# Reordering the start of a fused gated cross-attention and feed-forward kernel: first scores behind half of the projections, weight sums behind the scores, all of w_o held back

## The chip, the cores and the metric

The kernel runs on one core of a Trainium2 chip. The metric is device time in microseconds, as the median of several executions. One more execution was profiled by the hardware; its own time and its span (first to last instruction) are given beside each other below. The matrix engine is called PE, the vector engine DVE, the scalar engine ACT, GpSimd POOL, and the queue that issues most DMAs SP.

## What is computed

There are 16 batches of 224 tokens with 512 channels. Each batch has 750 context rows of 384 channels, of which a mask drops some. Cut to what matters:

```python
x = x + tanh(g0) * xattn(layernorm(x), ctx, mask)   # 8 heads of 64
x = x + tanh(g1) * ffn(layernorm(x))

def xattn(x, ctx, mask):
    q = x @ W_q;  k = ctx @ W_k;  v = ctx @ W_v      # split into heads
    p = softmax(where(mask, q k^T / 8, -max))
    return (p v) @ W_o + b_o

def ffn(x):                                          # 512 -> 2048 -> 512
    h = gelu(bitlinear(x, w1, b1))
    return bitlinear(h, w2, b2)

def bitlinear(x, w, b):
    s = 1 / mean(|w|)                                # one number for a whole matrix
    wq = clip(round(w * s), -1, 1) / s               # ternary weights
    return act_quant(rmsnorm(x)) @ wq.T + b
```

The ternary weights can only be formed when a whole matrix has been read, since their scale is the mean of its absolute values.

## The kernel before

The kernel ranks the batches by how many context rows the mask keeps, and gathers only those rows (at most 192 for a batch of the first half, 128 for the second). A batch in this order has a number `s` from 0 to 15. The path that runs is `compact_path`; its pieces, with their lines:

- `fetch` and `gather` (L936, L848) are indirect DMAs, issued by POOL, for token rows and context rows. `select(s)` (L807) makes the row numbers of batch `s`: six comparisons on DVE (`ind`, L814), twelve small matmuls (`pi`, L820), two conversions on DVE (`keys`, L831).
- `norm(i)` (L942) normalises two tiles of 128 tokens: statistics on DVE (`bs_x`, `mv_x`, L950 and L951), the rest on POOL (L954 to L959). The first two tiles have their own form, `norm_first` (L963).
- `query_pieces(s)` (L997) holds the transposes `turn` (`xnp`, L985) and two halves of the query projection (`qp_0`, `qp_2`, L1006). `context_pieces(s)` (L865) holds two transposes (`ctxp`, L879), two halves of the key projection (`kp_0`, `kp_2`, L890), the values (`vp`, L905) and the values of the rows past 128 (`vr`, L916). A result in PSUM is copied out by `evict` (L755), on DVE (L761) or ACT (L764), whichever has less planned work by a running estimate, `load`.
- `scores(s, n)` (L1035) is a quarter of a batch's scores: four matmuls `sim` (L1045), a masked maximum for each head on DVE (L1059), an exponential on ACT (L1069), a reciprocal on DVE (`rec`, L1078), a product on POOL (L1079). Quarters 0 and 1 need only the first half of the queries and of the keys. `turn_probs` (L1089) transposes the result (`ptp`, `ptr`), and `weighted` (L1113) applies it to the values.
- The weights: `load_weights` (L1338) brings w1 in eight pieces of 512 KB; w2 follows piece by piece into the same buffers as these come free. `sum_weights` (L1352) sums the absolute values of a piece, even ones on DVE (`wsums`, L1359), odd ones on ACT (`junk`, L1363). `scale_weights` (L1367) adds the eight sums (`wtot`, L1369), spreads the total by a matmul (`wtotp`, L1371) and makes the scale `sw`. `round_weights` (L1388) makes a ternary piece in three passes of DVE (L1392, L1393, L1394), and `turn_weights` (L1397) transposes it (`wp`, L1405 for w1, L1409 for w2).
- `late_loads` (L229) loads b_o, b2, W_o and b1 by SP. A copy of one element into a destination, made by ACT after the last weight sum (L1482 and L1483), holds such a load back until w1 has been summed. Of W_o, only the piece in slots 0 and 1 (L236) is held so; slots 2 and 3 (L237 and L238, 256 KB each) are not.

Every engine runs its instructions in the order of its own queue. That order is made when the program is built: a scheduler takes instructions in the order in which the Python code names them, and lets one pass another where it believes it to be ready sooner. `tc.issue_after(ins)` puts what is named inside the block behind `ins` on the queue of `ins`'s engine. It adds no wait on another engine.

The start of the work is written out by hand; from then on `merge` (L1430) interleaves three streams by estimated cost: the attention of batch `s`, the preparation of batch `s + 1`, and either the weights (s = 0 for w1, s = 1 for w2) or the feed-forward of finished token tiles.

Of the kernel before, what the change touches and what calls it, by code (L numbers as in the profile page):

```python
# [725 lines left out]
def compact_path(ctx, tc, sh, x, context, out, late_loads):  # L726

    nc = tc.nc
    P = 128
    B, S, D = x.shape  # L730
    _, J, C = context.shape
# [20 lines left out]

    load = {"v": 0.0, "s": 0.0}

    def evict(dst, src, cols):  # L755

        kind = {"saturate": False} if dst.dtype == F8 else {}
        v, s = 80 + 1.2 * cols, 90 + 1.0 * cols
        if load["v"] + v <= load["s"] + s:
            load["v"] += v  # L760
            nc.vector.tensor_copy(dst, src, **kind)  # L761
        else:
            load["s"] += s
            nc.scalar.copy(dst, src, **kind)  # L764

    def gen(shape, dtype, name):
        return ps_gen.tile(shape, dtype, tag="gen", name=name)
# [36 lines left out]
    def rows_of(s, t):  # L804
        return min(CAPS[s] - t * P, P)

    def select(s):  # L807

        st = live[s]
        cap = CAPS[s]  # L810
        nt = 2 if cap > P else 1
        ind = pa.tile([TJ, NJ, 192], BF16, tag="ind", name=f"ind_{s}", bufs=1)
        for n in range(NJ):
            nc.vector.tensor_scalar(ind[:, n, :cap], sh.place[:TJ, :cap], sh.upto[:, n, s : s + 1], None, ALU.is_ge)  # L814
        load["v"] += 6 * 170
        pi = gen([P, 2], F32, f"pi_{s}")
        for t in range(nt):
            rows = rows_of(s, t)
            for n in range(NJ):
                nc.tensor.matmul(  # L820
                    pi[:rows, t : t + 1],
                    lhsT=ind[:, n, t * P : t * P + rows],
                    rhs=sh.one[:, 0:1],
                    start=(n == 0),
                    stop=(n == NJ - 1),
                )

        keys = pa.tile([P, 2], I32, tag="keys", name=f"keys_{s}", bufs=3)
        for t in range(nt):
            rows = rows_of(s, t)  # L830
            nc.vector.tensor_scalar(  # L831
                keys[:rows, t : t + 1],
                pi[:rows, t : t + 1],
                float(J - 1),
                sh.first[:rows, s : s + 1],
                ALU.min,
                ALU.add,
            )
        st["keys"] = keys

        mb = pa.tile([TQ, 320], F32, tag="mask", name=f"mask_{s}", bufs=1)
        nm = 320 if nt > 1 else P
        nc.vector.tensor_scalar(
            mb[:, :nm], sh.place_f[:TQ, :nm], sh.slots[:TQ, 0, s : s + 1], -FMAX, ALU.is_ge, ALU.mult
        )
        st["mask"] = mb
# [18 lines left out]
    def context_pieces(s):  # L865
        st = live[s]
        cap = CAPS[s]
        nt = 2 if cap > P else 1

        def trans(c0, c1):  # L870
            if c0 == 0:
                st["ctxT"] = pa.tile([P, NC, 192], F32, tag="ctxT", name=f"ctxT_{s}", bufs=1)
                st["kT"] = pa.tile([P, NP, 320], F32, tag="kT", name=f"kT_{s}", bufs=2)
                st["v"] = pa.tile([P, D], F32, tag="v", name=f"v_{s}", bufs=2)
            pt = gen([P, c1 - c0, cap], F32, f"ctxp_{s}_{c0}")
            for c in range(c0, c1):
                for t in range(nt):
                    rows = rows_of(s, t)
                    nc.tensor.transpose(  # L879
                        pt[:, c - c0, t * P : t * P + rows],  # L880
                        st["ctx"][:rows, t, c * P : (c + 1) * P],
                        ident[:rows, :rows],
                    )
            evict(st["ctxT"][:, c0:c1, :cap], pt, (c1 - c0) * cap)

        def keys(p0):
            pk = gen([P, 2, cap], F32, f"kp_{s}_{p0}")
            for p in (p0, p0 + 1):
                for c in range(NC):
                    nc.tensor.matmul(  # L890
                        pk[:, p - p0, :],
                        lhsT=sh.wk[:, c, p * P : (p + 1) * P],
                        rhs=st["ctxT"][:, c, :cap],
                        start=(c == 0),
                        stop=(c == NC - 1),
                    )
            evict(st["kT"][:, p0 : p0 + 2, :cap], pk, 2 * cap)
            if cap > P:

                evict(st["kT"][DH:, p0 : p0 + 2, 192:], pk[DH:, :, :P], 2 * P)  # L900

        def values():
            pv = gen([P, D], F32, f"vp_{s}")
            for c in range(NC):
                nc.tensor.matmul(  # L905
                    pv, lhsT=st["ctxT"][:, c, :P], rhs=sh.wv[:, c, :], start=(c == 0), stop=(c == NC - 1)
                )
            evict(st["v"], pv, D)

        def values_rest():  # L910

            pv = gen([P, NP, DH], F32, f"vr_{s}")
            for c in range(NC):
                by = sh.wv[:, c, :].rearrange("p (i j d) -> p i j d", j=2, d=DH)
                for j in range(2):
                    nc.tensor.matmul(  # L916
                        pv[j * DH : (j + 1) * DH],
                        lhsT=st["ctxT"][:, c, P:],
                        rhs=by[:, :, j, :],
                        start=(c == 0),  # L920
                        stop=(c == NC - 1),
                    )
            st["v_rest"] = pa.tile([P, NP, DH], F32, tag="v_rest", name=f"v_rest_{s}", bufs=2)
            evict(st["v_rest"], pv, D // 2)

        pieces = [(0.5 * nt, lambda: trans(0, 2)), (0.3 * nt, lambda: trans(2, 3))]
        pieces += [(0.01 * cap, lambda p=p: keys(p)) for p in (0, 2)]
        pieces.append((1.5, values))
        if nt > 1:
            pieces.append((0.8, values_rest))  # L930
        return pieces
# [65 lines left out]
    def query_pieces(s):  # L997
        st = live[s]

        def query(p):  # L1000
            if p == 0:
                st["qT"] = pa.tile([P, NP, S], F32, tag="qT", name=f"qT_{s}", bufs=2)
            pq = gen([P, 2, S], F32, f"qp_{s}_{p}")
            for i in range(2):
                for d in range(ND):
                    nc.tensor.matmul(  # L1006
                        pq[:, i, :],
                        lhsT=sh.wq[:, d, (p + i) * P : (p + i + 1) * P],
                        rhs=st["xnT"][:, d, :],
                        start=(d == 0),  # L1010
                        stop=(d == ND - 1),
                    )
            evict(st["qT"][:, p : p + 2, :], pq, 2 * S)

        pieces = [(0.4, lambda t=t: turn(t)) for t in tiles_of(s)]
        pieces += [(3.0, lambda p=p: query(p)) for p in (0, 2)]
        return pieces
# [5 lines left out]
    def norm_pieces(s):  # L1023
        pieces = []
        for t in tiles_of(s):
            if t % 2 == 0:
                pieces.append((0.0, lambda t=t: norm(t // 2)))
                if t // 2 + 2 < NTOK // 2:
                    pieces.append((0.0, lambda t=t: fetch(t // 2 + 2)))
        return pieces  # L1030
# [302 lines left out]
    NPC = FF * D // P // W  # L1333
    sh.isw = [None, None]
    raws = {}
    weight_sums = []
# [15 lines left out]
    def sum_weights(wi, c):  # L1352
        if c == 0:
            weight_sums.append(pa.tile([P, NPC], F32, name=f"wsums_{wi}"))
        if c == 1:
            late["junk"] = pa.tile([P, FF], F32, tag="h", name=f"junk_{wi}", bufs=2)
        raw = raws[wi, c]
        if c % 2 == 0:
            nc.vector.tensor_reduce(  # L1359
                weight_sums[wi][:, c : c + 1], raw, AX.X, ALU.add, apply_absolute_value=True  # L1360
            )
        else:
            nc.scalar.activation(late["junk"][:, :W], raw, AF.Abs, accum_out=weight_sums[wi][:, c : c + 1])  # L1363
# [106 lines left out]
    with tc.issue_after(load_weights(0, 0)):  # L1470
        for c in range(1, NPC):
            load_weights(0, c)
    for piece in query_pieces(0) + context_pieces(0):
        piece[1]()
    for _, piece in norm_pieces(1):
        piece()
    select(2)
    for c in range(NPC):
        sum_weights(0, c)
    scale_weights(0)  # L1480

    for dst in (sh.wo[0:1, 0, 0:1], sh.bo[0:1, 0:1], sh.b1[0:1, 0:1], sh.b2[0:1, 0:1]):  # L1482
        nc.scalar.copy(dst, weight_sums[0][0:1, NPC - 1 : NPC])  # L1483
    late_loads(True)
    scores(0, 0)
    scores(0, 1)

    begun = 0
    for s in range(B):
# [30 lines left out]
    while begun < NPAIR + 2:  # L1520
# [7 lines left out]
        c = up_pieces(i - 1) if i - 1 < NPAIR else []  # L1528
# [34 lines left out]
```

## Time and profile before

| What | Value |
|---|---|
| median of 3 runs | 779.38 us (778.71 to 779.67) |
| the profiled execution: its own time, its span | 781.03 us, 779.2 us |
| mean granted PE clock in it | 0.947 |
| PE busy | 698.1 us, 90% of the span |
| DVE busy | 514.6 us, 66% |
| ACT, POOL busy | 387.4 us (50%), 370.9 us (48%) |
| DMA moved | 58.76 MB, 75 GB/s over the span |

The profile is a page with six parts: busy times; the span in 40 slices of 19.5 us, with a digit for the busy tenths of each engine and for the granted PE clock; DMA queues; the chain of work that ended last; the costliest groups of instructions; DMA issues. From the same trace come lists: the timeline of an engine (start, duration, engine, line, operation, result, operands, count, and in brackets the idle time before it and what ended it; several instructions in a row are merged, with the count as x8), the chain in order of time (start, length, what), the waits of a window, and tables of busy time by window. An fp32 matmul of the program appears as two records. Times are from the start of the span.

### The profile page before, as it was taken

Reading aid. Unit: us, or ns where it says so; the run is one execution under the profiler, and the core shown is the slowest. Engines: PE = TensorE matmul, PEld = TensorE weight load, DVE = VectorE, ACT = ScalarE, POOL = GpSimd, SP = SyncE. Lnnn points to the kernel's source line nnn. Section 1 sums busy time; section 2 is a strip of 40 time slices with the busy share of each in tenths; the row PEclk is TensorE's granted clock in tenths of the full one; section 3 lists DMA queues with packets and bytes.
Section 4 is the critical chain, followed back from the end, with each engine's and each line's share of the span. In section 5 each row is a group of like instructions: output and inputs, shape, how many; then the busy total and the mean of one; then the engine's idle time right before and its main releaser. Section 6 shows DMA issues by size and latency. Waiting matters only on the chain.

```text
span 779.2 us, 11250 instructions
## 1 busy us (share of the span) xinstructions
PE 698.1 (90%) x3902; PEld 446.6 (57%) x3902; DVE 514.6 (66%) x1293; ACT 387.4 (50%) x947; POOL 370.9 (48%) x468
## 2 busy tenths in 40 slices
PE   3698799999998998998999889999998999989762
PEld 2566587666564664664756476666564756443321
DVE  5479774758657539536687825695858576688960
ACT  1248664354826527346374654382728364554330
POOL 6446358453563453535537433555362425254331
PEclk9889989999999798998999979999999999999886
DMA  6855122111311223024133310242312222223331
GB/s 218 299 178 173 33 67 58 30 43 29 82 44 44 73 68 77 16 69 91 41 70 84 90 36 11 69 92 68 66 54 58 53 55 55 68 55 90 83 85 45
DMA packets 87185, 58.76 MB, mean 75 GB/s; under 512 B 75456, under 2 KB 75600, under 8 KB 86992
## 3 DMA queue, kind: packets, MB, share of 16 engines
q1 hardware_dynamic: 78992, 32.00, 18.2%
q0 software_dynamic: 8128, 25.96, 10.6%
q8 instruction: 33, 0.54, 0.3%
q14 instruction: 32, 0.26, 0.1%
HBM read 32.26 MB, written 7.34 MB: 51 GB/s over the span
## 4 chain that ended last, share of the span: by engine, by line
PE 67%; DVE 16%; ACT 5%; issue 4%; DMA 3%; POOL 2%; DVEq 0%; POOLq 0%; ACTq 0%; SPq 0%
PE qp L1006 12%; PE hp L1257 10%; PE fp L1303 10%; PE kp L890 8%; PE op L1187 7%; DVE a L1280 4%; PE vp L905 4%; PE av L1124 4%; PE sim L1045 3%; DVE hq L1283 3%; DVE h L1265 3%; PE ptp L1099 3%; DMA raw<-in_L_ffn_w_dram 2%; ACT h L1277 1%; ACT p L1069 1%
## 5 line engine op out<-in xcount | busy, mean ns | idle before, releaser
L1079 POOL TENSOR_TENSOR p<-p,rec 112x768 f32<-112x768 f32 (+1 forms) x64 | 81.3, 1273 | 151.9 <-DVE rec L1078 99.3
L1265 DVE SCALAR_TENSOR_TENSOR h<-hp,c,b_bc 128x1024 f32<-128x1024 f32 x56 | 71.6, 1281 | 95.2 <-PE hp L1257 95.2
L1257 PE MATMUL hp<-w1T,xqT 128*128 128x512 fp8e4 x448 | 108.7, 389 | 8.0 <-DMA xqT<-xq 5.1
L1069 ACT ACTIVATE p<-p,nm 112x192 f32<-112x192 f32 (+1 forms) x256 | 106.5, 421 | 17.2 <-DVE nm L1059 17.1
L1187 PE MATMUL op<-wo_sb,xoT 128*128 128x512 f32 x224 | 107.4, 618 | 3.3 <-DVE y L1190 3.2
L1303 PE MATMUL fp<-w2T,hqT 128*128 128x512 fp8e4 x448 | 103.0, 386 | 7.5 <-DMA hqT<-hq 7.5
L1006 PE MATMUL qp<-xnT,wq_sb 128*128 128x224 f32 x512 | 106.7, 364 | 2.4 <-ACT xnT L764 2.4
L1006 PEld LDWEIGHTS qp<-xnT,wq_sb 128*128 128x128 f32 x512 | 98.4, 197 | 5.6 <-ACT xnT L764 3.1
L1059 DVE CUSTOM_DVE_ANT_0 p<-sim,mask 112x192 f32<-112x192 f32 (+1 forms) x256 | 69.1, 316 | 24.1 <-PE sim L1045 22.0
L1257 PEld LDWEIGHTS <-xqT 128*128 128x128 bf16 x448 | 43.2, 99 | 64.8 <-issue 18.5
L1303 PEld LDWEIGHTS <-hqT 128*128 128x128 bf16 x448 | 43.9, 99 | 60.5 <-DMA hqT<-hq 9.0
L890 PE MATMUL kp<-ctxT,wk_sb 128*128 128x192 f32 (+1 forms) x384 | 68.3, 330 | 7.9 <-issue 6.0
L1277 ACT ACTIVATE h<-h 128x2048 f32<-128x2048 f32 x28 | 53.5, 1911 | 42.7 <-DVE h L1265 27.6
L890 PEld LDWEIGHTS kp<-ctxT,wk_sb 128*128 128x128 f32 x384 | 62.5, 211 | 15.5 <-issue 8.9
L1045 PE MATMUL sim<-kT,qT 64*112 64x192 f32 (+1 forms) x512 | 56.8, 327 | 12.7 <-DVE nm L1059 12.6
L1187 PEld LDWEIGHTS op<-wo_sb,xoT 128*128 128x128 f32 x224 | 41.9, 197 | 44.9 <-issue 39.1
L1280 DVE TENSOR_REDUCE a<-h 128x1 f32<-128x2048 f32 x28 | 63.6, 2280 | 5.0 <-ACT h L1277 4.9
L791 POOL DMA_INDIRECT x<-in_x_dram,token x28 | 33.8, 1206 | 59.6 <-PE xnp L985 42.0
L1045 PEld LDWEIGHTS sim<-kT,qT 64*112 64x112 f32 x512 | 39.0, 178 | 32.1 <-DVE nm L1059 15.2
L1289 ACT ACTIVATE sq<-h 128x2048 bf16<-128x2048 f32 x28 | 53.1, 1899 | 7.6 <-DMA hqT<-hq 7.6
L764 ACT COPY kT<-kp 128x256 f32<-128x256 f32 (+2 forms) x43 | 17.4, 405 | 79.3 <-PE kp L890 71.3
L764 ACT COPY qT<-qp 128x448 f32<-128x448 f32 x31 | 16.5, 533 | 72.7 <-PE qp L1006 72.7
(167 smaller groups left out, 1161.0 us busy)
## 6 DMA issues: line engine op xcount, KB each, us to landing
raw<-in_L_ffn_w_dram SPq DMA_DIRECT2D x16, 512.0 KB, 4.9
wq_sb<-in_L_xattn_W_q_dram SPq DMA_DIRECT2D x1, 1024.0 KB, 5.7
b_bc<-in_L_ffn_b_dram SPq DMA_DIRECT2D x1, 1024.0 KB, 8.6
wk_sb<-in_L_xattn_W_k_dram SPq DMA_DIRECT2D x1, 768.0 KB, 7.3
wv_sb<-in_L_xattn_W_v_dram SPq DMA_DIRECT2D x1, 768.0 KB, 8.7
wo_sb<-in_L_xattn_W_o_dram SPq DMA_DIRECT2D x2, 256.0 KB, 4.0
wo_sb<-in_L_xattn_W_o_dram SPq DMA_DIRECT2D x1, 512.0 KB, 3.8
x<-in_x_dram,token POOLq DMA_INDIRECT x28, 4.8
```

The lines of the kernel that those rows point to most:

```text
L890: nc.tensor.matmul(pk[:, p - p0, :], lhsT=sh.wk[:, c, p * P : (p + 1) * P], rhs=st["ctxT"][:, c, :cap], start=(c == 0), stop=(c == NC - 1),)
L1006: nc.tensor.matmul(pq[:, i, :], lhsT=sh.wq[:, d, (p + i) * P : (p + i + 1) * P], rhs=st["xnT"][:, d, :], start=(d == 0), stop=(d == ND - 1),)
L1045: nc.tensor.matmul(sim[:, j, i, :cap], lhsT=st["qT"][j * DH : (j + 1) * DH, p, q * TQ : (q + 1) * TQ], rhs=st["kT"][j * DH : (j + 1) * DH, ...
L1059: nc.vector.tensor_tensor_reduce(out=probs[:, h, :cap], in0=sim[:, j, i, :cap], in1=st["mask"][:, j * begin : j * begin + cap], scale=-(DH ...
L1069: nc.scalar.activation(probs[:, h, :cap], probs[:, h, :cap], AF.Exp, bias=nmax, scale=-1.0, accum_out=total[:TQ, h : h + 1],)
L1079: nc.gpsimd.tensor_tensor(probs[:, :, :cap], probs[:, :, :cap], rec[:TQ].unsqueeze(2).to_broadcast([TQ, 4, cap]), ALU.mult,)
L1187: nc.tensor.matmul(po, lhsT=xoT[:, d, at : at + P], rhs=sh.wo[:, d, :], start=(d == 0), stop=(d == ND - 1))
L1257: nc.tensor.matmul(ph[:, n, :], lhsT=f["xqT"][:, k * ND + d, :], rhs=w1T[:, d, at : at + NB], start=(d == 0), stop=(d == ND - 1),)
L1265: nc.vector.scalar_tensor_tensor(h[:, cols], ph.rearrange("t i n -> t (i n)"), f["c1", k], sh.b1[:, cols], ALU.mult, ALU.add)
L1277: nc.scalar.activation(f["h", k], f["h", k], AF.Gelu)
L1280: nc.vector.tensor_reduce(amax[:, k : k + 1], h, AX.X, ALU.max, apply_absolute_value=True)
L1303: nc.tensor.matmul(po, lhsT=f["hqT", k][:, n, :], rhs=w2T[:, n, :], start=(n == 0), stop=(n == NF - 1))
```

## The change

It touches the hand-written start of `compact_path`. `evict` notes the latest eviction on DVE and on ACT. The context transposes of batch 0 come ahead of the token transposes. Then come the first half of the queries and the first half of the keys. All else of the start is queued, on DVE and ACT, behind the latest eviction of each: the two quarters of scores, then the second halves, the values, the sums of w1 and its scale, the normalisation of the next two tiles, the selection for batch 2. Two more one-element copies hold back the other two loads of W_o.

```diff
+    latest = {}
+
     def evict(dst, src, cols):
...
-            nc.vector.tensor_copy(dst, src, **kind)
+            latest["v"] = nc.vector.tensor_copy(dst, src, **kind).ins
...
-            nc.scalar.copy(dst, src, **kind)
+            latest["s"] = nc.scalar.copy(dst, src, **kind).ins
...
-    for piece in query_pieces(0) + context_pieces(0):
-        piece[1]()
-    for _, piece in norm_pieces(1):
+    queries, keys_values = query_pieces(0), context_pieces(0)
+    for _, piece in keys_values[:2] + queries[:2]:
         piece()
-    select(2)
-    for c in range(NPC):
-        sum_weights(0, c)
-    scale_weights(0)
-
-    for dst in (sh.wo[0:1, 0, 0:1], sh.bo[0:1, 0:1], sh.b1[0:1, 0:1], sh.b2[0:1, 0:1]):
-        nc.scalar.copy(dst, weight_sums[0][0:1, NPC - 1 : NPC])
+    for _, piece in queries[2:3] + keys_values[2:3]:
+        piece()
+
+    with ExitStack() as behind:
+        for instruction in latest.values():
+            behind.enter_context(tc.issue_after(instruction))
+        scores(0, 0)
+        scores(0, 1)
+        for _, piece in queries[3:] + keys_values[3:]:
+            piece()
+        for c in range(NPC):
+            sum_weights(0, c)
+        scale_weights(0)
+        for _, piece in norm_pieces(1):
+            piece()
+        select(2)
+
+        held = [sh.wo[0:1, 0, 0:1], sh.wo[0:1, 2, 0:1], sh.wo[P // 2 : P // 2 + 1, 2, 0:1]]
+        for dst in held + [sh.bo[0:1, 0:1], sh.b1[0:1, 0:1], sh.b2[0:1, 0:1]]:
+            nc.scalar.copy(dst, weight_sums[0][0:1, NPC - 1 : NPC])
     late_loads(True)
-    scores(0, 0)
-    scores(0, 1)
```

The queues of the two built programs, compared, differ in these places (before, then after):

- DVE, from the normalisation of tile 1 on. Before: six `ind` of batch 2, `bs_x` of tiles 2 to 5 mixed with `wsums`, the eviction of `ctxp_0` behind five of these six `bs_x` and two `wsums`, the evictions of the keys, `wtot`, the rest of `select(2)`, `sw`, the eight maxima of the scores, the six `ind` of batch 3, the first rounding. After: the eviction of `kp_0`, two `wsums`, the eight maxima, `rec`, a `wsums`, the eviction of `qp_2`, a `wsums`, `rec`, two evictions of `kp_2`, `wtot`, two `bs_x`, six `ind`, the eviction of `vr`, `sw` mixed with two `bs_x`, `keys` and six `ind`, the first rounding.
- PE. Before: `xnp`, `qp_0`, `qp_2`, `ctxp`, `kp_0`, `kp_2`, `vp`, `vr`, `pi`, `wtotp`, `sim` of quarters 0 and 1. After: `ctxp`, `xnp`, `qp_0`, `kp_0`, two matmuls of `qp_2`, `sim` of quarters 0 and 1, the rest of `qp_2`, `kp_2`, `vp`, `vr`, `wtotp`, `pi`.
- ACT. Both evictions of `ctxp` come first; the exponentials of quarter 0 stand ahead of `junk` of piece 5, those of quarter 1 ahead of `junk` of piece 7 and of the one-element copies.
- POOL. The products of quarters 0 and 1 come ahead of the normalisation of tiles 2 and 3, the gather of batch 2 and the two products of biases and gates (L1502, L1503), rather than behind them.
- SP. The loads L237 and L238 move from ahead of w1 to behind b_o and b2, still ahead of b1.
- Later, up to the fourth batch, some ten evictions change between DVE and ACT or change places by a few; after that the queues are the same.

## Prediction, made before the changed kernel ran

> **What bounds the kernel now.** I read first the slices of the page, then the chain in order of time, then the timelines of DVE and PE, then windows.
>
> ```profile
> PE   3698799999998998998999889999998999989762
> PEclk9889989999999798998999979999999999999886
> ```
>
> A digit is a slice of 19.5 us. PE is the bound from the sixth slice to the last three. Below nine it is in the first, second, fourth and fifth: 0 to 97 us. Time saved there stays saved if what follows is bound by PE.
>
> In the chain (start, length, what) the worst place is this:
>
> ```profile
> 32.77 2.89 issue
> 35.66 6.60 PE kp L890 x24
> 42.26 2.58 PE vp L905 x6
> 44.84 1.45 PE vr L916 x12
> ```
>
> PE idles 5.98 us before the keys. Its operand `ctxT` comes from DVE, whose timeline says why it is late:
>
> ```profile
> 30.93 0.69 DVE L950 BATCH_NORM_STATS2 bs_x<-x 128x6 f32<-128x512 f32 x1 [2.42 <-DMA x<-in_x_dram,token]
> 32.69 0.69 DVE L950 BATCH_NORM_STATS2 bs_x<-x 128x6 f32<-128x512 f32 x1 [1.06 <-DMA x<-in_x_dram,token]
> 33.30 1.20 DVE L1359 TENSOR_REDUCE wsums<-raw 128x1 f32<-128x1024 f32 x1
> 34.42 0.68 DVE L950 BATCH_NORM_STATS2 bs_x<-x 128x6 f32<-128x512 f32 x1
> 35.02 0.54 DVE L761 COPY ctxT<-ctxp 128x384 f32<-128x384 f32 x1
> ```
>
> PE made `ctxp` by 29.7. The copy stands behind statistics of later tiles, and these wait for their rows. Then the clock (columns: window, length, busy PE, PEld, DVE, ACT, POOL, granted clock, DMA share, GB/s):
>
> ```profile
> 30.00:35.60 5.60, 0.00 (x0) 0.00 (x0) 3.60 (x6) 1.42 (x4) 1.52 (x2) 0.84 0.85 330
> 35.60:37.60 2.00, 1.94 (x6) 1.97 (x7) 1.68 (x2) 0.00 (x0) 0.00 (x0) 0.50 0.04 8
> 39.60:41.60 2.00, 2.00 (x10) 2.00 (x10) 1.68 (x2) 0.37 (x1) 0.00 (x0) 0.73 0.00 0
> ```
>
> So the keys run at half clock: 24 records take 6.60 us, where 12 take 2.05 at full clock (the chain at 104.25). From 50.84 on DVE is full with rounding w1:
>
> ```profile
> 50.84 0.75 DVE L1392 TENSOR_SCALAR raw<-raw,sw 128x1024 f32<-128x1024 f32 x1
> ...
> 56.69 1.95 DVE L1393 TENSOR_SCALAR w<-raw 128x1024 int16<-128x1024 f32 x1
> 58.56 1.95 DVE L1392 TENSOR_SCALAR raw<-raw,sw 128x1024 f32<-128x1024 f32 x1
> ```
>
> ```profile
> 56.46 3.50 POOL L1079 TENSOR_TENSOR p<-p,rec 112x768 f32<-112x768 f32 x2
> ```
>
> ```profile
> 62.00:78.00 16.00, 12.71 (x82) 9.46 (x81) 16.00 (x36) 13.59 (x36) 9.26 (x8) 0.89 0.59 179
> 97.00:117.00 20.00, 19.84 (x127) 17.34 (x126) 14.46 (x32) 13.13 (x29) 11.19 (x11) 0.87 0.24 66
> ```
>
> DVE is busy 16.00 of 16 us to 78 us; PE takes over by 97. PE also waits 3.29 us at 70.66 for `p` from POOL.
>
> **What the Trainium skill says.** "TensorE: Matmul & The Clock Gate", section "What's actually happening", says that PE's clock is halved after an idle window of about 3.4 us and released after as much sustained work. The trace agrees: 0.50 after 5.98 us idle, 0.73 in the window from 39.6. "SBUF — State Buffer", section "Who interferes with whom", says that DVE's copies and tensor_scalar operations in two-port modes and POOL lock each other out. The trace agrees: L1393 takes 1.95 us beside POOL's product, against 0.67 at 54.34. The same section says that tensor_reduce never does so; `wsums` takes 1.20 to 1.22 us everywhere here.
>
> **The change, part by part.** Sums are against the profiled execution (781.03 us, span 779.2); the median of the runs, 779.38, is 1.65 below it, and I subtract the same saving from both.
>
> Step 1, up to the first half of the queries. `ctxp` (1.40 us) now precedes `xnp` on PE. The second context gather is issued at 14.45 and such a gather lands in about 3.0 us: 17.5. `ctxp` may so hold `xnp` (17.70 before) back by 0.5 us. Against this, 0.5 MB of W_o leaves the DMA engines between 9 and 13 us, at some 350 GB/s 1.4 us of them, and rows of x may land up to 0.9 us sooner. I take 0, from -0.9 to +0.5. `qp_0` then ends as before, when ACT copies it (25.45): 25.4.
>
> Step 2, keys without the stall. `ctxT` is now copied by ACT, idle then. `kp_0` follows at full clock, since PE has worked since 17.7: 12 records, 2.05 us, to 27.45. If half clock persisted it would be 3.3 (half of 6.60), the upper end. DVE copies it in 0.55, ACT the rest in 0.37: 28.4. PE fills this with four records of `qp_2`.
>
> Step 3, PE from there. `sim` 1.5 (to 30.0), rest of `qp_2` 12 x 0.19 = 2.3, `kp_2` 2.05, `vp` 2.6, `vr` 1.5: 38.5, where before 46.28 and `sim` still to come. PE is thus 9 us ahead; but it then needs ternary weights, so DVE decides.
>
> Step 4, DVE. DVE's queue now begins with the copy of `kp_0`: all behind it, 5.9 us of statistics, comparisons and sums that lay in idle time, waits until 27.45 and comes after. With starts of successive rows: copy 0.55, two `wsums` at 1.13 (30.3), eight maxima 2.3 (32.6; 48.12 to 50.42 before), `rec` 0.1, `wsums` (33.85), `qp_2` 0.5, `wsums` (35.5), `rec` (ACT's exponentials from 30.7: 4 x 0.44, `junk` 1.16, 4 x 0.44, so 35.4), `kp_2` 0.55 and 0.4 (36.5), `wtot` (ACT's last `junk` ends at 36.6) 36.8. Then two `bs_x` 1.25, `ind` 1.27 with aggregates, `vr` 0.42, `sw` chain 0.35, two `bs_x` 1.25, `keys` 0.32, `ind` 1.27, aggregate 0.1: 6.3. First rounding at 43.1 against 50.84: -7.7. No DMA is late: the chain has the raw pieces there by 31.6 and DMA falls to 0.04 by 35.6. Two statistics of tiles 6 and 7 move past the rounding, 1.2 us; DVE idles 1.38 us before 85.00, so they cost 0, and 1.2 without that cover.
>
> Step 5, the products. The first two of POOL (3.50 us) now come at 32.7 and 35.6, beside `wsums` and copies from PSUM, not beside rounding: the two rows of 1.95 return to 0.67 and 0.75, -2.5. In exchange the biases' products (2.62 and 2.35 alone at 51.5 to 56.5 before) and the normalisation of two tiles stay beside rounding; rows beside these were 1.09 for 0.74 and 0.82 for about 0.5, so +0.7. Together -1.8.
>
> Step 6, the wait at 70.66. POOL's four gathers before it (63.83 to 69.11) follow the evictions and come at about 52 to 57; `rec` comes at 43.1 + 13.1 = 56.2, `p` at 58.8. PE gets there at 46.1 + 12.9 = 59.0. The 3.29 us vanish on PE, but DVE's later pieces are next late, so I book nothing; it is the upside, about 2 us.
>
> Step 7, queues moved past. Three loads of W_o (1 MB) and the three others now go by SP at 36.9, behind ACT's six copies of 0.1 us, done by 46; the next on SP, w2, waits for a rounding at 45 anyway, and DMA's share was 0.16 from 35.7 to 48.6. W_o is needed at 126. Normalised tile 2 moves from 31.6 to about 41, needed by PE at about 43. The evictions that change engine later: 0, within 1 us either way.
>
> Sum: -7.7 - 1.8 = **-9.5**. From 97 us PE is full and all shifts alike. 781.03 - 9.5 = 771.5 profiled; median **769.9**.
>
> **Rivals.** *The products still collide and half clock persists over `kp_0`*: step 5 gives 0, step 2 loses 1.25, step 1 loses 0.5: -6.0, 773.4. For it: POOL's queue shifts by as much as DVE's. Against: the products stand ahead of the weights in both queues.
>
> *The weights stay where they were*: if w1's sums end as late as before, because of DMA or PE's `wtotp` behind `vr`, only the 2.5 us of step 5 are won, less 1.0 of noise: -1.5 or less, 778. Against: `raw` is there by 34.5; `wtot` waited for ACT, not DMA.
>
> *DVE's head of queue makes it slower.* The copy of `kp_0` blocks everything on DVE. Rounding starts 15.65 us after it; gain and loss meet when 15.65 less 1.8 of step 5 reaches 50.84, that is with `kp_0` ending at 37.0 rather than 27.45. With wq or context rows late and PE at half clock for 16 + 12 records it could end at 39: +2, 781.4. Against: wq landed at 7 us and `qp_0` ended at 25.4.
>
> *More*: PE never waits at 70.66 and DVE keeps up: -11.5, 767.9.
>
> **Numbers.** Forecast 0.60, collision 0.20, more 0.08, weights stay 0.05, slower 0.07. A measurement of this kernel can tell 0.2% (1.6 us) from no change. Range 766.5 (step 1 and the upside both full: -9.5 - 0.9 - 2 is 767.0, less 0.5) to 775.5 (the collision with another 2 us of displaced statistics not covered). Faster 0.88, same 0.05, slower 0.07.
>
> **What would show it.** Right: no PE gap from 20 to 39 us; `kp_0` in about 2.1 us at clock 1; first L1392 near 43; L1393 near 0.67 there; first `wp` near 46; the same order from 97 on, 9 to 10 us earlier. Wrong: rounding starting after 46, rows of 1.95 still there, a new PE gap before `wp` of over 5 us, or the shift at `op` (126.39 before) differing from that at the end.

## The result, and the profile after

The changed kernel takes **770.83 us** (median of 4 runs, 770.80 to 770.91) beside 779.43 us for the kernel before (4 runs, 778.71 to 779.67): ratio 0.9891 (changed over before), 95% interval 0.9874 to 0.9908. The forecast was 769.9. The profiled execution of the changed kernel has its own time 770.80 us, at its median, and a span of 769.1 us. That of the kernel before took 781.03, which is 1.60 above the median of these four runs, so the two profiled executions differ by 10.2 us and the medians by 8.6.

Two lines are added above the functions concerned, so every line number is 2 higher than before. The slices first, of the changed kernel (19.2 us each):

```profile
PE   4999799999998998989999799999998999989762
PEclk9999899999997998997999889999999999999987
```

The second slice has gone from 6 to 9: PE is now busy for nine tenths or more of each slice from 19 to 77 us. What is left below nine is the first slice and the fifth. Then PE's timeline from 16 to 31.4 us:

```profile
16.34 2.01 PE L881 MATMUL ctxp<-ident,ctx 128*128 128x128 f32 x6 [3.74 <-DMA ctx<-in_ctx_dram,keys]
...
20.82 6.02 PE L1008 MATMUL qp<-xnT,wq_sb 128*128 128x224 f32 x16 [0.57 <-ACT xnT L766]
26.68 2.11 PE L892 MATMUL kp<-ctxT,wk_sb 128*128 128x192 f32 x12
...
29.53 1.86 PE L1047 MATMUL sim<-kT,qT 64*112 64x192 f32 x16
```

Of the rows shown only the first two have a bracket: the keys follow the queries without a gap, where PE idled 5.98 us before, and 12 records take 2.11 us, where they took about 3.3 (half of 6.60). The windows of the changed kernel (columns as in the prediction):

```profile
30.00:35.60 5.60, 5.60 (x39) 5.36 (x39) 5.53 (x21) 5.57 (x17) 1.41 (x1) 1.00 0.85 323
35.60:37.60 2.00, 2.00 (x7) 1.00 (x6) 1.97 (x5) 2.00 (x8) 0.62 (x2) 1.00 0.01 3
...
62.00:78.00 16.00, 15.21 (x133) 10.34 (x129) 13.35 (x36) 13.38 (x30) 3.22 (x2) 1.00 0.33 100
```

From 30 to 37.6 us PE, DVE and ACT are all but full and the clock is 1.00 (0.50 in the second window before). DVE, which had 16.00 of 16 us from 62 to 78, has 13.35. Its timeline shows the head of its queue and the first rounding:

```profile
28.83 0.56 DVE L763 COPY kT<-kp 128x384 f32<-128x384 f32 x1 [10.41 <-PE kp L892]
...
43.85 0.73 DVE L1394 TENSOR_SCALAR raw<-raw,sw 128x1024 f32<-128x1024 f32 x1
...
49.21 0.67 DVE L1395 TENSOR_SCALAR w<-raw 128x1024 int16<-128x1024 f32 x1
49.81 0.74 DVE L1394 TENSOR_SCALAR raw<-raw,sw 128x1024 f32<-128x1024 f32 x1
```

DVE waits 10.41 us for the first keys, and still rounds at 43.85 where it rounded at 50.84. The last two rows are the two passes that took 1.95 us each in the kernel before, at 56.69 and 58.56. POOL's first two products have moved away from the rounding:

```profile
34.19 1.46 POOL L1081 TENSOR_TENSOR p<-p,rec 112x768 f32<-112x768 f32 x1 [6.01 <-DVE rec L1080]
37.03 1.47 POOL L1081 TENSOR_TENSOR p<-p,rec 112x768 f32<-112x768 f32 x1 [1.38 <-DVE rec L1080]
```

(The later products still collide in both kernels: a cast beside one takes 2.20 us at 58.82 here and took 2.12 at 68.79.) Later on PE come the wait for the products and the first transposes of w2. In the kernel before:

```profile
70.66 0.60 PE L1099 MATMUL ptp<-ident,p 112*128 112x112 f32 x4 [3.29 <-POOL p L1079]
...
95.98 1.03 PE L1409 MATMUL wp<-ident,w 128*128 128x128 bf16 x8 [3.57 <-DVE w L1394]
```

In the changed kernel:

```profile
60.77 0.60 PE L1101 MATMUL ptp<-ident,p 112*128 112x112 f32 x4 [0.90 <-POOL p L1081]
...
85.39 1.03 PE L1411 MATMUL wp<-ident,w 128*128 128x128 bf16 x8 [3.57 <-DVE w L1396]
```

The first `op` comes at 115.59 rather than 126.32; the span ends 10.1 us earlier. So the gain is made before 86 us and kept.

### The profile page after: what moved, and what is told of

Its sections match the earlier page's. It is cut to its first block, busy times and chain, and to the rows that moved or that the text cites. A ratio compares the mean times of both kernels' runs of the same rounds, so it can differ in the third digit from the quotient of the medians.

```text
span 769.1 us, 11249 instructions
## 1 busy us (share of the span) xinstructions
PE 697.0 (91%) x3902; PEld 445.7 (58%) x3902; DVE 510.1 (66%) x1295; ACT 387.3 (50%) x947; POOL 372.3 (48%) x468
## 3 DMA queue, kind: packets, MB, share of 16 engines
q0 software_dynamic: 8128, 25.96, 10.7%
## 4 chain that ended last, share of the span: by engine, by line
PE 66%; DVE 17%; ACT 5%; issue 4%; POOL 3%; DMA 2%; DVEq 0%; POOLq 0%; ACTq 0%; SPq 0%
PE qp L1008 13%; PE hp L1259 11%; PE fp L1305 10%; PE op L1189 8%; PE kp L892 7%; DVE a L1282 4%; PE av L1126 3%; PE vp L907 3%; DVE hq L1285 3%; DVE h L1267 3%; PE sim L1047 3%; PE ptp L1101 3%; ACT p L1071 2%; ACT h L1279 1%; DVE p L1061 1%
## 5 line engine op out<-in xcount | busy, mean ns | idle before, releaser
L1061 DVE CUSTOM_DVE_ANT_0 p<-sim,mask 112x192 f32<-112x192 f32 (+1 forms) x256 | 69.2, 316 | 19.2 <-PE sim L1047 17.2
L892 PE MATMUL kp<-ctxT,wk_sb 128*128 128x192 f32 (+1 forms) x384 | 66.7, 325 | 1.8 <-ACT xnT L766 1.8
L766 ACT COPY pT<-ptp 128x448 f32<-128x448 f32 x63 | 33.4, 538 | 41.1 <-PE ptp L1101 41.0
```

Source lines behind the costliest of these rows:

```text
L892: nc.tensor.matmul(pk[:, p - p0, :], lhsT=sh.wk[:, c, p * P : (p + 1) * P], rhs=st["ctxT"][:, c, :cap], start=(c == 0), stop=(c == NC - 1),)
L1061: nc.vector.tensor_tensor_reduce(out=probs[:, h, :cap], in0=sim[:, j, i, :cap], in1=st["mask"][:, j * begin : j * begin + cap], scale=-(DH ...
```

## The experiments

Twelve runs were made, on three chips; the kernel before took 779.16, 779.74 and 779.69 us on these. Start times in us from each profile, and the median of the timed runs, are below. A ratio is to the kernel before on the same chip, with its 95% interval; it is estimated from all timed runs and need not be that of the two medians.

| run | first keys copied (by DVE) | first rounding | `wp` of w2 | `op` | `op` to end | median |
|---|---|---|---|---|---|---|
| before | 39.88 | 50.84 | 95.98 | 126.32 | 652.9 | 779.43 |
| changed | 28.83 | 43.85 | 85.39 | 115.59 | 653.5 | 770.83 |
| e1 w_o held | 40.05 | 51.57 | 96.29 | 125.45 | 652.4 | 779.62 |
| e2 context first | 32.33 (by ACT) | 46.30 | 89.25 | 119.41 | 649.2 | 771.03 |
| e3 w_o not held | 27.82 | 43.74 | 87.90 | 117.44 | 649.2 | 770.09 |
| e4 not behind | 34.76 | 52.99 | 96.06 | 126.14 | 653.1 | 779.99 |
| r1 changed | 28.36 | 43.39 | 85.62 | 115.26 | 649.0 | 769.94 |
| r2 context first | 30.69 (by ACT) | 44.86 | 87.74 | 117.28 | 648.9 | 770.35 |
| w1 fill at start | 25.89 | 44.63 | 88.29 | 117.44 | 655.0 | 770.24 |
| x2 no products | 39.23 | 49.72 | 92.36 | 121.95 | 648.5 | 773.35 |
| d1 delay 9 us | 38.06 | 53.39 | 95.05 | 124.08 | 652.0 | 781.67 |
| d2 delay 4 us | 33.16 | 48.48 | 90.13 | 119.35 | 652.5 | 776.27 |
| w5 fill before w2 | 28.03 | 43.17 | 85.26 | 113.39 | 650.7 | 768.61 |
| r3 changed | 27.46 | 43.23 | 87.41 | 116.96 | 652.2 | 769.61 |

The column "`op` to end" is the span less the start of `op`. From `op` on the work is the same in all, yet it takes 648.5 to 655.0 us. That goes with the clock PE was granted: with means of 0.93, 0.97, 0.95 and 1.00 in the windows 220 to 320, 320 to 420, 420 to 520 and 520 to 620 us (r1) it is 649.0, with 0.91, 0.95, 0.95 and 0.98 (changed) 653.5; both are the same kernel. r3, that kernel again, takes 652.2, neither of the two values that were expected of it, with 0.93, 0.95, 0.95 and 0.98. Over the whole stretch, averaged from windows of 100 us, the clock is lowest in w1 (0.958, for 655.0 us) and highest in r1 and r2 (0.970, for 649.0 and 648.9), and the other eleven profiles lie between these in the same order to within 1 us. A single profile therefore says more of an edit by its `op` than by its end.

**e1, only W_o held.**

```diff
-    for dst in (sh.wo[0:1, 0, 0:1], sh.bo[0:1, 0:1], sh.b1[0:1, 0:1], sh.b2[0:1, 0:1]):
+    for dst in (sh.wo[0:1, 0, 0:1], sh.wo[0:1, 2, 0:1], sh.wo[P // 2 : P // 2 + 1, 2, 0:1], sh.bo[0:1, 0:1], sh.b1[0:1, 0:1], sh.b2[0:1, 0:1]):
```

> The kernel before, with one edit: the two other loads of W_o are held back as in the changed kernel; order of the start as before. Theory (the gain is the removed stall of PE before the keys and, after it, the products that no longer stand beside the rounding): W_o is worth nothing, because the keys still wait for the copy of ctxp on DVE, and that waits for rows that land at 33 us: 779 us, within 1 us of before. Rival (W_o took DMA time ahead of the first rows of x, and the changed kernel's first statistics came at 13.1 us rather than 14.8): 1.5 us or more faster, 777.9 or less.

Measured 779.62, ratio 1.0003 (0.9985 to 1.002). Nothing, on its own.

**e3, the changed kernel without holding slots 2 and 3 of W_o.**

```diff
-        held = [sh.wo[0:1, 0, 0:1], sh.wo[0:1, 2, 0:1], sh.wo[P // 2 : P // 2 + 1, 2, 0:1]]
+        held = [sh.wo[0:1, 0, 0:1]]
```

> The changed kernel, with one edit: the two other loads of W_o are not held, so that they run at 9 to 13 us as before. Theory: the first rows of x land 1 to 1.7 us later, but PE's first work waits for the second context gather (17.1 us), so 0 to 1 us slower: 770.8 to 771.8. Rival (W_o counts): 772.3 or more.

Measured 770.09, ratio 0.9889 (0.9856 to 0.9921), as the changed kernel. Holding back all of W_o counts for nothing within what these runs can tell (some 2.5 us either way).

**e2 and r2, only the context first.** In the kernel before, the context transposes come ahead of the token transposes; then both halves of the queries, then of the keys, and all else in the old order.

```diff
-    for piece in query_pieces(0) + context_pieces(0):
+    keys_values = context_pieces(0)
+    for piece in keys_values[:2] + query_pieces(0) + keys_values[2:]:
         piece[1]()
```

> The kernel before, with one edit: the two context transposes of batch 0 come ahead of its queries. Scores, sums, statistics and W_o stay as before. Theory: the copy of ctxp falls to ACT, the stall of 6 us and the half clock of the keys go, and PE reaches the first scores 6 to 7 us earlier; POOL's first products still stand beside the rounding, so their 2.5 us stay: 773 us (772 to 774.5), that is 6 to 7 of the 8.6 us. Rival A (the order of scores, sums and statistics on DVE brings most): 776 or more. Rival B (the stall is all, the rest brings nothing): 771.5 or less.

Measured 771.03, ratio 0.9898 (0.9868 to 0.9928). By time this is rival B (771.5 or less), not the theory (772 to 774.5), but the interval reaches into both; the edit was run again on another chip, with the changed kernel beside it (r1). The expectation of r2 calls the first result "between the two theories", which it was not, and describes the edit wrongly in one point: all the queries, not half, come before the keys.

> The kernel before with one edit: the context transposes of batch 0 come first, then half of the queries and of the keys; all else of the start in its old order. Its first run gave 771.0, between the two theories. Theory: the weights of w2 arrive 6.5 us earlier than in the kernel before and the changed kernel's 10 us earlier, so 773, 2 us above the changed kernel beside it. Rival: within 1 us of the changed kernel, so that the order of scores and sums that the change adds to it is worth nothing in time.

> The changed kernel once more, on the same chip as the next three, so that its distance to the version that has only the context transposes first is known on one chip. Theory (scores ahead of the weight sums, and the first two products of POOL away from the rounding, are worth another 2 to 3 us at the first rounding and about 1.8 us beyond): 770.8 on a chip where the kernel before takes 779.3, range 769.5 to 772; the version with the context first alone is 1.5 to 3.5 us above it. Rival (that part counts nothing in the end): the two lie within 1 us.

Measured r2 770.35, ratio 0.9888 (0.9865 to 0.991); r1 769.94, ratio 0.9875 (0.9853 to 0.9897). By time the two are 0.4 us apart, and e3 and e2 0.9: the rival's "within 1 us", though the intervals are each 3.5 us wide and more and allow the theory's 2. By these two pairs of profiles it is 2.0 us: `op` at 115.26 and 117.28 (r1, r2), at 117.44 and 119.41 (e3, e2), and the spans differ by the same, 764.3 and 766.2, 766.6 and 768.6. By `op`, r2 has 9.0 of r1's 11.1 us, and e2 6.9 of e3's 8.9: some four fifths of the gain or more comes from the two lines of e2. That the rest is worth 2 us isn't shown: r3, the same kernel as r1, has its `op` at 116.96, only 0.3 before r2's.

That two lines suffice hangs on what `evict` makes of them: in e2 and r2 the copy of the first keys falls to ACT, where nothing waits for rows ahead of it. ACT of r2:

```profile
30.69 0.48 ACT L764 COPY kT<-kp 128x384 f32<-128x384 f32 x1 [2.21 <-PE kp L890]
```

In e4, below, the context comes first too, and that copy falls to DVE. What r2 still lacks of the changed kernel is seen on its DVE and POOL:

```profile
44.86 2.72 DVE L1392 TENSOR_SCALAR raw<-raw,sw 128x1024 f32<-128x1024 f32 x2
...
50.46 1.68 DVE L1394 CAST w<-w 128x1024 bf16<-128x1024 int16 x1
```

```profile
45.06 1.89 POOL L1079 TENSOR_TENSOR p<-p,rec 112x768 f32<-112x768 f32 x1
...
49.97 1.89 POOL L1079 TENSOR_TENSOR p<-p,rec 112x768 f32<-112x768 f32 x1
```

Two passes of 0.74 take 2.72 together and one of 0.41 takes 1.68, each beside a product. The changed kernel no longer has this collision of the first two products.

**e4, the changed kernel with its order of the code, but nothing put behind the evictions.**

```diff
         for instruction in latest.values():
-            behind.enter_context(tc.issue_after(instruction))
+            pass
```

> The changed kernel, with one edit: nothing is queued behind the latest evictions; the code names the pieces in the same order, and the scheduler places them. On DVE four statistics and two sums of weights so come ahead of the copy of kp_0, and two more statistics before the first maxima. Theory: that copy comes at about 34 us rather than 28.8, since the statistics wait for rows, PE stops for some 4 us before the first scores, but fewer statistics are left for later; the first rounding starts at about 45.5 rather than 43.85: 772.5 us (771.5 to 774). Rival (statistics in DVE's idle time are worth more than early scores): 770 or less.

Measured 779.99, ratio 1.0009 (0.9993 to 1.0025). The whole gain is gone, where 2 us less was expected: a miss by 7.5. DVE of e4 says why:

```profile
33.03 0.69 DVE L952 BATCH_NORM_STATS2 bs_x<-x 128x6 f32<-128x512 f32 x1 [1.86 <-DMA x<-in_x_dram,token]
33.64 1.20 DVE L1361 TENSOR_REDUCE wsums<-raw 128x1 f32<-128x1024 f32 x1
34.76 0.55 DVE L763 COPY kT<-kp 128x384 f32<-128x384 f32 x1
```

and PE of e4:

```profile
27.16 2.11 PE L892 MATMUL kp<-ctxT,wk_sb 128*128 128x192 f32 x12
...
35.45 1.59 PE L1047 MATMUL sim<-kT,qT 64*112 64x192 f32 x4 [4.29 <-DVE kT L763]
...
38.01 2.90 PE L1047 MATMUL sim<-kT,qT 64*112 64x192 f32 x12
```

The keys leave PE at 29.3 (28.8 in the changed kernel), but their copy on DVE stands behind statistics that wait for rows, as `ctxT` did in the kernel before. PE waits 4.29 us for it and then works at half clock (0.50 in the windows from 34 to 42 us; 12 records of `sim` in 2.90, against 16 in 1.86). The stall has only moved one step on. What keeps it out of the changed kernel is that nothing that waits for rows stands ahead of that copy.

**x2, the kernel before without the first two products.**

```diff
+        if s > 0 or n > 1:
             nc.gpsimd.tensor_tensor(
...
```

> The kernel before without POOL's product of probabilities and reciprocals for the first two quarters of batch 0 (that normalisation is left out of the result); nothing else changes in any queue. It prices the collision of step 5 by itself. Theory: the two passes of 1.95 us at 56.7 and 58.6 return to about 0.7, the ternary pieces, w2 and op come 2 to 2.5 us earlier, and the time falls by 1.5 to 2.5 us to about 777.2. Rival: the DVE is given the two microseconds, but the next wait takes them (for the product at 70.66, or for the pieces of w2), op comes at most 0.7 us earlier and the time stays within 0.7 us of the kernel before.

Measured 773.35, ratio 0.9937 (0.9915 to 0.9958), that is -4.9 us with -6.6 to -3.3 (-6.4 by the medians). More than expected. From the first rounding to `wp` of w2 it takes 42.64 us rather than 45.14, the 2.5 us of step 5. But first rounding itself is 1.1 earlier, before any product, and `op` to end is 4.4 shorter: neither can come from the edit. By `op`, less that 1.1, it is -3.3. The edit also shortens POOL's queue, and the wait of 3.29 us at 70.66 goes with it; on PE of x2 the same transposes start at 67.46 without a bracket. The two passes of 1.95 us take 0.67 and 0.74 there. So the collision is worth 2.5 us, and x2 can't tell how much of the other 0.8 is the wait at 70.66.

**d1 and d2, doses of delay.** Between `qp_0` and `kp_0` of the changed kernel, matmuls nobody reads (`fill`: 128x512 fp32, ones by w_q): ten in d1, five in d2. `latest["q"]` is here the last matmul of `qp_0`.

```diff
-    for _, piece in queries[2:3] + keys_values[2:3]:
-        piece()
+    queries[2][1]()
+    with tc.issue_after(latest.pop("q")):
+        delay = fill("delay", 10)
+    with tc.issue_after(delay):
+        keys_values[2][1]()
+    latest.pop("q", None)
```

> The changed kernel with ten matmuls whose results nobody uses (128x512 fp32, some 0.91 us each, as those of vp) on PE between qp_0 and kp_0: the first half of the keys comes 9.1 us later, and the copy of kp_0 at the head of DVE's queue starts at about 37.9 rather than 28.8. It tests the break-even of the rival that DVE's head of queue decides (kp_0 ending at 37.0 by the prediction). Theory: all that DVE does up to the rounding moves one for one, first rounding at about 52.9, and what is left of the gain is step 5 and the wait for the products: op 0 to 2 us before that of the kernel before, the time within 2 us of it, 777.5 to 780. Rival (the delay is absorbed in part, by the pieces of w1 that land late or by PE's waits further on): the first rounding comes before 50 and the time stays 4 us or more below the kernel before.

> The same with five such matmuls, 4.5 us. Theory, one for one: first rounding at about 48.4, op at about 120, the time 4 to 5 us above the changed kernel beside it. Rival (absorbed in part): first rounding before 46.5, the time less than 2.5 us above the changed kernel.

Measured d1 781.67, ratio 1.0011 (0.9989 to 1.0032); d2 776.27, ratio 0.9951 (0.9928 to 0.9974). Both times lie above their forecasts (777.5 to 780, and 4 to 5 us above the changed kernel). The copy at the head of DVE's queue in d1:

```profile
38.06 0.56 DVE L763 COPY kT<-kp 128x384 f32<-128x384 f32 x1 [18.88 <-PE kp L892]
```

Up to the rounding it is one for one: with the copy at 28.83, 33.16 and 38.06 rounding starts at 43.85, 48.48 and 53.39, that is 15.0, 15.3 and 15.3 later, and `op` comes at 115.59, 119.35 and 124.08. Nothing absorbs the delay before the rounding; of 4.6 and 9.5 us there, 3.8 and 8.5 are left at `op`. With the keys at 38 us the gain is gone by time, while `op` is still 2.2 ahead. The times of d1 lie 774.5 to 785.6, and d2's median is 6.7 above r3 where its `op` is 2.4 above that of r3 and 4.1 above that of r1; what the doses cost beyond `op` stays open, but for d1 it goes with the clock: its ten executions with a mean granted clock of 0.957 or more, the profiled one among them, took 774.5 to 780.7, the twelve with 0.953 or less 779.1 to 785.6.

**w1, PE kept busy before the first queries.** Two such matmuls between the row numbers of batch 1 and the first transposes; `pi_last` is the last matmul of `select(1)`.

```diff
+    with tc.issue_after(live[1]["pi_last"]):
+        fill("start", 2)
```

> The changed kernel with two matmuls whose results nobody uses, 128x512 fp32, on PE between the row numbers of batch 1 (12.6 us) and the first transposes (16.3 us), so that PE isn't idle for 3.7 us there. The 16 records of qp_0 took 6.02 us at half clock where 16 records take 3.1 to 3.3 us later. Theory (the idle stretch halved the clock): qp_0 takes 3.0 to 3.3 us, kp_0 ends at about 26 rather than 28.8, the first rounding comes 2 to 3 us earlier unless the pieces of w1 bound it, and the time falls by 1 to 2.5 us to 768.5 to 770. Rival (nothing before qp_0 decides, since the row sums of w1 wait for ACT or for the pieces that land at 31 to 34 us): qp_0 is quicker, but the first rounding stays within 0.7 us of 43.9 and the time within 0.7 us of the changed kernel's.

Measured 770.24, ratio 0.9885 (0.9867 to 0.9903): by time the rival, though the first rounding comes 0.8 us later than in the changed kernel's first profile, just past the 0.7 that the rival allowed. The profiled execution was the slowest of the seven (774.14). PE of w1:

```profile
13.33 3.74 PE L1464 MATMUL fill_start<-wq_sb,ones 128*128 128x512 f32 x4
...
20.60 3.29 PE L1008 MATMUL qp<-xnT,wq_sb 128*128 128x224 f32 x16 [0.62 <-ACT xnT L766]
...
42.33 2.90 PE L1047 MATMUL sim<-kT,qT 64*112 64x192 f32 x14
```

`qp_0` takes 3.29 us rather than the 4.69 to 6.02 of the seven other profiles with this queue, so the idle time before it was the cause of its half speed. The keys come 2.9 us sooner, and nothing is won. DVE of w1:

```profile
35.77 1.22 DVE L1361 TENSOR_REDUCE wsums<-raw 128x1 f32<-128x1024 f32 x1 [1.51 <-DMA raw<-in_L_ffn_w_dram]
...
47.86 0.34 DVE L833 TENSOR_SCALAR keys<-pi,first 128x1 int32<-128x1 f32 x2 [2.49 <-PE pi L822]
```

The row sums now wait for the pieces of w1 (which were also issued 0.7 us later than in the changed kernel's profile, at 17.35 against 16.70). And PE, ahead of its work, idles from 36.9 to 40 but for 0.35 us, falls to half clock (0.50 in the windows from 42 to 48), takes 2.90 us for 14 records of `sim` that took 1.55, and so delivers `pi` late: DVE waits 2.49 us for row numbers in the middle of the rounding.

**w5, PE kept busy before w2.** Four matmuls nobody reads in the 3.57 us that PE waits for the first ternary piece of w2.

```diff
         w16 = quantised.pop((wi, c))
+        if wi == 1 and c == 0:
+            fill("w2", 4)
```

> The changed kernel with four matmuls whose results nobody uses (128x512 fp32) on PE just before the first transposes of w2 (wp at 85.4), where PE waits 3.57 us for the first ternary piece of w2 and then works at half clock until about 91 (wp 1.03 us for 8 records that take 0.61 at full clock). They take 3.6 us, about the wait. Theory (the idle stretch halves the clock, and PE is the bound soon after): wp takes 0.6, the keys after it 2.1 per 12 records, op comes 1 to 2.5 us earlier, and the time falls by 1 to 2.5 us below the changed kernel beside it. Rival (DVE's rounding of w2 bounds that stretch, so that PE's half clock costs nothing): the wp and keys are quicker, but op and the time stay within 0.7 us.

> The changed kernel once more, beside the three others on one chip, as their reference: 770 to 771 where the kernel before takes 779.5. If the spread after op comes from the granted clock alone, its stretch from op to the end is again near 649 or near 653.5 us, and the difference follows the granted clock in the windows from 120 on.

Measured w5 768.61, ratio 0.9858 (0.9834 to 0.9881); r3 769.61, ratio 0.9848 (0.9818 to 0.9879). PE of w5:

```profile
85.26 0.62 PE L1413 MATMUL wp<-ident,w 128*128 128x128 bf16 x8
...
86.62 2.15 PE L892 MATMUL kp<-ctxT,wk_sb 128*128 128x192 f32 x12
```

The mechanism is as the theory has it: 0.62 and 2.15 us, where r3 has 1.04 and 3.16, and from `wp` of w2 to `op` 28.1 us against 29.6 in r1 and r3 and 30.2 in the changed kernel's first profile (29.0 to 30.3 in all the other profiles). That is 1 to 2 us. By time it is 1.0 below r3 by the medians and above it by the ratios, which each rest on six runs: not separable. It is the best of the versions by its profile, not proved so by its times.

r3 is worth a look for another reason. Its `qp_0` took only 4.69 us and its keys came 1.4 us sooner than in the first profile; its `op` came 1.4 later. On PE:

```profile
40.73 2.90 PE L1047 MATMUL sim<-kT,qT 64*112 64x192 f32 x14
```

and on DVE:

```profile
46.27 0.34 DVE L833 TENSOR_SCALAR keys<-pi,first 128x1 int32<-128x1 f32 x2 [2.30 <-PE pi L822]
```

It is the same as in w1, without any edit: the granted clock is 0.50 from 42 to 46 us (1.00 in the first profile), `pi` is late, DVE waits 2.30 us for it. Between `vr` and these 14 records PE has only one-column matmuls (`wtotp`, `pi`) and two records of `sim`, and the `pi` stand behind comparisons on DVE. When PE comes sooner, that stretch is longer: 2.3 us in r3 (38.4 to 40.7) and 2.5 in e3, which both fall to half clock, 1.6 to 1.8 in r1, w5, d1, d2 and in the first profile, which don't (there DVE waits 0.30 to 0.41). PE's busy share in it is still 0.90 in r3 and 0.84 in e3, so that it is this thin stretch that sets the clock down is only argued. Its price is seen: some 2 us, by which DVE waits longer and r3 and e3 stand behind r1 at `op`.

## Why the prediction was right, step by step

The forecast was 769.9, the median 770.83; the profiled execution was to be 771.5 and is 770.80.

*Step 1, queries: no change.* Short by 1.4 us: `qp_0` ended at 26.8, not 25.4. It started at 20.82 as forecast (20.73 before). Its rows had landed 1.7 us sooner (first statistics at 13.07, 14.75 before), which won nothing, since `xnp` now stands behind `ctxp`; in e3, with the rows at 14.74, it started at 21.02. But it took 6.02 us, and its length varies in the same kernel from 4.69 to 6.02. Even the upper end of the bound, +0.5, was too low. The prediction took the speed of `qp_0` from one profile and didn't ask why 16 records took some 4.7 us there. w1 answers that: idle time before it.

The Trainium skill has the rest: "TensorE: Matmul & The Clock Gate", section "What's actually happening", says that the cold stretch is run-variable, because the window by which the hardware judges is free-running. The 4.69, 5.62 and 6.02 us of `qp_0` in three profiles of one kernel agree; the prediction cited the section and left that sentence out of its bound.

*Step 2, keys without the stall at full clock.* Right: no gap, 2.11 us (forecast 2.05).

*Step 3, PE 9 us ahead.* `vr` ended at 39.8, forecast 38.5; the difference is step 1's 1.4.

*Step 4, first rounding -7.7.* Measured -7.0. From the copy of the keys to the first rounding the listed rows gave 15.65; measured 15.02 here, 15.0 to 15.9 in the seven profiles with this queue and unlike starts (all but w1). So the sum was 0.6 too long, which hid part of step 1's 1.4. This sum over DVE's queue is the part of the prediction that carried it, and d1 and d2 show that it is a chain without slack. The rival *DVE's head of queue makes it slower* put its break-even at keys ending at 37.0; d1, with them ending at 38.0, measured 1.0011 (0.9989 to 1.0032). e4, where a late copy of the keys on DVE takes the whole gain, is akin to that rival.

*Step 5, the products, -1.8, and step 6, the wait at 70.66, 0 with an upside of 2.* From first rounding to `wp` of w2 it was 45.14 us and is 41.54, so the two together give -3.6 (-2.9 in r1, the same kernel; 44.18 us in r3, with its late row number). The rows of 1.95 are gone; x2 gives -2.5 for the collision. How the other 1.1 us divides isn't shown. On PE the waits of 0.90 and 0.79 us are what is left of 3.29, 1.6 less. But in the kernel before DVE was busy 16.00 of 16 us around that wait, so the wait held up nothing on DVE there, and `wp` waits for DVE. The passes of the rounding in this stretch (L1392 to L1394) take 24.8 us before and 21.8 in the changed kernel, so step 5 was booked too small at least in part; they don't decide alone, for in r1 they take 20.4. The two steps made up for the 0.7 that was missing at the first rounding, and more. The forecast was right in sum, with terms off in opposite senses: the mechanism was right, but that the sum came so near is in part luck.

*Step 7, queues moved past, 0.* Right for the loads of W_o (e1, e3); what else moves was not tested by itself.

*From 97 us on all shifts alike.* `wp` of w2 -10.6, `op` -10.7, end -10.1. Right, but for the granted clock after `op`.

The sum on the profile was -9.5 and is -10.2. *The weights stay where they were* and *the products still collide* are refuted by the first rounding and by POOL's timeline. What the medians give less than the profiled pair, 1.6 us, is the one execution of the kernel before that was profiled above its median. The prediction subtracted its sum from both. By the medians the changed kernel is 8.6 us ahead here, 9.8 in r1 and 10.1 in r3.

What it did not see is how the gain divides. It puts the sum down to the whole change; e2 and r2 show that the context transposes alone can bring all but 0 to 2 us, and e4 that they bring nothing where the copy of the keys is then late on DVE. And it took PE coming sooner for a gain or nothing, where r3 and w1 show that it can cost 2 us.

## What to carry to other kernels

When an engine stands idle, look at what stands ahead of the late instruction on the queue of the engine that releases it; here a copy of 0.54 us stood behind statistics that waited for rows, and most of the gain came with taking that copy and the next, that of the keys, out from behind them (e2, r2). Where only the first copy is mended, the next on the same queue is late and the gain is gone (e4), so follow the chain to the work that must be done. Add up such a queue row by row: if there is no slack in it, a delay at its head costs its full length where the queue ends its work (the first rounding in d1 and d2), and a gain at its head counts only until another wait, a load or a clock, takes over (w1).

## What had not been expected

- Sixteen records of `qp_0` took 3.29 us with PE busy since 13.3 us and 4.69 to 6.02 without, in the changed kernel. The granted clock in the windows from 21 to 26 us is given as 1.00 in all of these: there only the durations show the half speed, and the loads at 400 GB/s beside it are the same in w1 (408).
- PE coming 1.4 us sooner went with an `op` 1.4 us later (r3 against the first profile): half clock in the `sim` of the next quarters, a late row number, 2.30 us of waiting on DVE.
- After `op`, the same work took 648.5 to 655.0 us, in step with the granted clock.
